# A GpSimd filler between row transfers, 128x256 or 128x512, with a new order of operations

## The chip, the core and the metric

The kernel runs on one core of one Trainium2 chip. The metric is the device time of one execution in microseconds (us). Seventeen executions of the kernel before the change have a median of 1318.66 us (1315.17 to 1323.75).

The engines are named as in the profile: PE is TensorE (matmuls), DVE is VectorE, ACT is ScalarE, POOL is GpSimd, and SP is the engine that issues the plain DMA transfers. Each engine works through its own queue of instructions in order and waits on semaphores for the others.

## What is computed

Two sequences of 2048 tokens with 128 features (4096 rows) go through a layer of the "macaron" kind: half a mixture of experts, a state-space block, half a mixture of experts.

```python
x = x + 0.5 * ffn(layernorm(x))      # mixture of experts, the first time
x = x + ssm(layernorm(x))            # selective state space: a scan over 2048 steps
x = x + 0.5 * ffn(layernorm(x))      # the same mixture, the second time

# ffn: 32 experts of 128x128, the 4 best of each row, and one shared expert of width 512
scores = softmax(flat @ router_w.T + router_bias)
topk_scores, topk_idx = top_k(scores, 4)
h = silu(flat @ gate_w[e].T) * (flat @ up_w[e].T);  out_e = h @ down_w[e].T
out = sum of the four chosen out_e, weighted with topk_scores
out = out + silu(flat @ sgate_w.T) * (flat @ sup_w.T) @ sdown_w.T

# ssm, 256 channels with 16 states each
h = h * exp(dt_t * A) + dt_t * u_t * B_t;  y_t = (h * C_t).sum(states) + D * u_t
```

## The kernel before

**Blocks and groups.** The 4096 rows are eight blocks of 512 rows, blocks 0 to 3 being the first sequence and 4 to 7 the second. A mixture takes groups of blocks: in the first mixture (0,1), (2,3) and (4,5,6,7), in the second (0,1,2,3), (4,5) and (6,7). Between them the state-space part goes through the blocks in order, since the states are carried on from block to block of a sequence.

**A mixture of a group.** DVE works out a place for each row at each of its four experts (the index tile `idx`, L855). POOL then scatters the rows to DRAM so that the rows of one expert lie together: an indirect DMA (L924) moves 128 rows at once, 4 x 4 of them for a block. These are the row transfers called *scatters* below; the DRAM tensors are `xs_100` for the first group of a layer's pair, `xs_102` and `xs_104` for the others. SP loads the sorted rows in chunks of 512 (`xs`, L1014), PE, ACT and DVE put each chunk through its experts (`pt_x` L1023, `gu` L1040, `h` L1065, `oq` L1078), and SP stores the result to DRAM (`ys`, L1091). Once all chunks of the group are stored, POOL *gathers* four results for each 128 rows into the tile `yg` (L1105, again an indirect DMA, 16 for a block), and PE adds them up with their weights (`sum`, L1130).

**A block of the state-space part.** After the projections, POOL forms `dt` and `dtu` in six products and sums of 128x512 (L1322 to L1324, called the *dt step* below, which waits for the logarithm of ACT at L1317). Then, for each of the 16 states, POOL multiplies `dtu` by a row of B (L1354, a *drive*, 128x1024), DVE scans twice (L1392) and multiplies by C (L1405), and PE adds the state up (L1171).

**The order.** Engines PE, DVE, ACT and SP run in the order in which the program is written out, and POOL's instructions are chained to the same order. That order is a list of 4504 operation numbers, `ORDER`, written into the file; `Plan.run` turns it into the order of emission. So the list decides what stands behind what in every queue.

**The filler.** Where more than two row transfers follow each other in POOL's order without other POOL work, `Plan.run` marks the third and every later one with `pause`, and `Plan.emit` then calls `pause()` ahead of it: POOL fills a tile named `pad`, which nobody reads, with zeros (L414). It is 128 partitions of 256 bf16 columns. There are 402 such fillers, called *pads* below.

Of the kernel before, what the change touches and what calls it, by code (L numbers as in the profile page):

```python
# [47 lines left out]
1 96 10 0 109 12 8 4-5 14 20 7 11 25 9 6 13 21 52 113 112 16 111 114-117 121-122 877 876 879 118-119 123-124 120  # L48
125-131 178 180 179 182-183 181 184-185 132 134 133 135-138 186-187 190 188-189 191-194 878 880 195 881 139 196-198
882 199 142 200 202 201 203-205 208 206 209 207 892 210 883 211 143 140 212 884 141 887 213 144-145 888-889 988-993  # L50
996 994-995 997 1000 998 1001 999 893 1002 894 1003 885 1004 39 18 26 22 17 24 19 15 98 27 29 28 23 40 46 34 2 94 3
73 79 72 93 85 35 48 32 104 59 31 45 44 63 110 88 82 77-78 49 102 494 56 92 84 886 1005 897 895-896 495 898-899 1006
1008 1007 1010-1011 1009 1012-1015 1018 1016 1019 1017 890 146 167 164 169 158 175 151 156 162 177 172-174 168 150
176 161 153 165 152 170 154 147-149 159 155 157 171 160 163 166 1020 900 1021-1022 496-497 891 901-902 498-499 903
1023 500 1024 1026 1025 1028-1030 904 906 1027 908 81 97 74-75 36 62 41 103 43 47 91 42 100 89 30 57 86 76 50 33 71
95 69 83 37 87 53 38 80 1031 905 907 909 108 214 90 105 228 242 70 51 68 215 442 216 106 66 256 1032-1033 1036 1034
1037 1035 1038-1039 910 912 1040 911 913-915 1041 217-220 229 221-223 230 224 243 916 244 231-232 225-226 233-235
257-258 917 236 245 237 246 238 247-248 259 249-250 260-261 239-240 270 64 58 61 227 241 60 67 284 65 298 251-252
262-264 560-562 271-272 253 563 920 265 254-255 266 273 276 285 274-275 277 286 267-268 278 921 279-280 287 290
288-289 291 281-282 292 918-919 922-923 293-294 299-300 54 312 326 269 564 295 566 296 503 565 567-568 570 569  # L60
572-573 571 574 504-505 575 501-502 301-302 506-507 303-304 313 305 327 306 314 307 576 508-511 328 512-513 308 577
315-316 318 317 340 354 368 283 309 319-320 310 341-342 514 321-322 516 515 517-518 578-579 582 580 583 581 519-520
584-587 590 588 591 589 592-593 521 329 332-333 330-331 334 594-595 55 382 311 297 323 355 324 356 335-336 343-348
369-370 337-338 325 396 339 101 349-350 357 360 358 361 359 362 351-352 363-364 1042-1045 524 1046 1048 1047
1049-1051 1054 1052 1055 1053 383 1056-1057 384 371 374 372-373 365 385 375 366 386 376-377 410 424 353 367 397
387-388 378 398 389 379 390 380 411 391 412 392 399-400 402 401 393 425 403 394 404-405 1058-1059 426 395 381 406
924 931 955 938 973 945 970 941 930 983 946 952 929 978 933 939 976 936 927 962 948 958-959 937 943 953 986 950 944
932 954 951 928 942 947 982 528 961 540 549 553 558 537 555 544 531 539 530 532 535 554 538 934 556 536 985 545 529
542 541 552 533-534 925 557 548 551 550 543 546 559 547 413 416 414-415 417-418 407-409 427 419 428-429 420 430-434
421 596 610 422 624 99 423 435-436 597 522-523 525 598 611-612 599-600 602 601 603-604 437 638 625-626 613 616  # L70
614-615 605 617-618 639 606-607 640 652 619 608 627-628 620 630-631 629 621 632 622 979 956 972 935 957 949 975 984
441 439-440 438 447-448 446 445 443 609 666 444 653 633 654 449 634 641 644 642-643 645-646 667-668 450-451 647-648
635 456 636 623 680 637 694 454 926 455 452-453 655 658 656 649 659 650 657 681-682 660-662 460 462 459 461 457-458
669 672 670-671 463 673 663 674 464 664 465 708 651 675 470 683-684 676 685-688 695 689 677 722 665 1508 696 690 678
1509-1510 691 709-710 692 1511-1512 467 977 468 476 466 474 473 981 475 469 940 697-699 1515 1513-1514 471 1516 472
700 477 701 1521 702 1522 703 723 1524 724 704 1528-1529 693 736 750 1523 764 679 478 1525-1526 711-712 479 714-715
713 1527 716 737-738 1530 705 717 706 1534 718 1535-1536 1531-1532 1542 707 778 1519 725 728 1537 526 1520 726 729
1538 968-969 967 965 487 490 489 482 481 488 971 483 480 1533 1539 1543 964 730 727 484 751-752 731 719-720 732
485-486 491 1544 492 527 493 1540 1545 739 742 740 1546 765 743 1547 741 744 766 1554 745-746 1548-1549 1555 721
1552 792 974 1553 1562-1563 733 1572-1573 963 753 756 1541 1556 734 754 1557-1558 755 757 735 806 758 1559 1564 1551  # L80
759 1565 1712 760 1550 779 747-748 780 1560 1566-1569 1574-1575 1582 749 1592 1517 767 770 1518 768 771 1576-1579
1584 769 772 1561 761-762 1586 1571 773 793 1585 774 1570 794 1602 1583 1593 1612 763 1587-1589 1594-1595 781
784-785 1580 782 1597-1598 807 1596 1581 1591 783 786 1599 1604-1605 808 1590 787 1600 788 775 1606 1603 980 1622
1632 795 1601 798 1607-1609 776 1614-1615 1613 1616-1619 1713 796 789 799 790 966 987 960 1060 777 1623 1633 1624
800 797 1611 801 1625 1714 809 1626-1629 812 1620 802 1610 1634-1635 1637-1638 803 1621 1636 1631 813 810-811 814
1639 1630 1644 804 1645 815-816 1642 1652 791 1662 1074 1646 1061-1062 1715 1643 817 1647-1649 1641 1075 1640 1654
1651 1653 1672 818 1657 1655 1658 1650 1716 1076 1664 1717 1665 1663 1667-1668 1674 1063 1656 1675 1673 1064 1659
1719 1666 1661 1677 1065 1669 1678 1718 1077 1720 1660 824 1078 1066-1067 1676 1068 1079 1088 805 1682 1692 819 1102
107 1679 1725 1732 1684 1670 1726 1685 1728 1069 1733 1070 1734 1683 823 829 820 830 821-822 828 827 1693 1686-1689
1727 1116 1746 1756 825 837 835 834 1071 1696 1671 1681 1089 1729 1694 1730 1735 1680 1736 1695 826 1072 1731 1090  # L90
831 1738 1697-1699 1766 1691 832 1737 836 1739-1740 1700-1701 1707-1708 1702-1703 1741-1742 838 833 842 1743 1747
841 843-844 1757 1709 1704 1080-1081 839-840 1082 1705 1710 845 1690 1748-1749 1706 1751 1711 1744 1758 1721 1723
1750 1745 1091 1752-1753 1722 1724 1092 1094 1754 1095 1759 1093 1761 1096 1767 1130 1776-1777 849-850 848 851
846-847 1083 852 1768 1916 1762 1103 1760 1763 1097 1084 1917 1769 1764 1098 1104 1918 1770-1773 1117 1755 1085 1765
1919 1778 1118 1779 1920 1086 1775 1780 1786 1796 1073 1787 1797 1781-1783 1788 1774 1789 1921-1923 1790 1105 1785
1791-1793 1924 1106 1798 1107 853 1799 1929 859 1930 1784 1794 854 1800-1803 1808 1936 1809 1932 1804 1937 1108 1810
1099-1100 1795 1806 1805 857 855 1807 1811-1813 1815-1817 858 1144 1826 1836 1931 1087 856 1818-1819 1933 1820-1823
1938 1119 1814 1934 1109 1120-1121 1939 1110 1935 1828 1111 1830 1827 860 1837 864 1101 1158 1846-1847 862 1942 1825
1829 1831-1833 861 1940 1112 1838 1131 1839 1824 1943-1944 1132 1840 1113-1114 1841-1843 1848-1849 1122 1133 1850
1145 1835 1845 1856 1941 863 865 1857 872 871 1851-1853 1945 1834 1134 1844 1123-1124 1135 1866 1115 1858 1125 1859  # L100
1946 1146 1126 1860-1863 1867 1876-1877 1868-1869 1871 1136 1855 1137 1127 1147 1870 1138 1150 1872-1873 1128 1148
1864 866 1854 1149 1151 867-868 1152 1878 1865 1159 1886 1172 1186 1879 1947-1948 1173-1174 1160 1139 1880 1896 1887
1153 1881-1883 1888 1140 1889 1874 1154 1884 1141 1890 1875 1891-1893 1142 1898 1161 1885 1900 1164 1899 873 869
1897 870 1901-1903 874 1894 1952 1950 1200 1951 1955 1162 1165-1166 875 1163 1904 1953 1895 1905 1954 1167 1175
1956-1957 1960 1129 1911 1906 1168 1962-1963 1178 1176 1179 1961 1970-1971 1214 1980 1143 1981 1965-1966 1177 1180
1972 1949 1155-1156 1990 1157 1964 1959 1967 1912-1913 1187-1188 1973 1181 1201 1974 1182 1202 1169 1975-1977 1968
1958 1982 1170 1983 1171 2000 2010 1228 1985-1986 1189-1190 1192 1907 1969 1193 1191 1194 1979 1984 1908 1987 1195
1992 1991 1995 2001 1196 1993 1996 1183 1215-1216 1184 1909 2002 1978 2005 1910 1197 1994 1203 1997 1206 1989 1400
# [1445 lines left out]
```

## Time and profile before

| what | value |
|---|---|
| median of 17 executions | 1318.66 us (1315.17 to 1323.75) |
| the profiled execution, its own time | 1320.99 us |
| its span, first to last instruction | 1319.2 us |
| mean granted TensorE clock in it | 0.91 |
| PE busy | 1051.9 us (80%) |
| POOL busy | 999.1 us (76%) |
| ACT busy | 896.8 us (68%) |
| DVE busy | 865.3 us (66%) |
| scatters, L924 (256) | 189.2 + 63.1 us, 985 and 986 ns each |
| gathers, L1105 (256) | 248.1 us, 969 ns each |
| pads, L414 (402) | 132.3 us, 329 ns each |
| drives, L1354 (128) | 303.3 us, 2380 ns each |

The shares of busy time are averages over stages with different limits. The first 300 us or so belong to the first mixture, whose experts of blocks 4 to 7 go on beside the state-space part; this one lasts from about 280 to 1030 us, with the second mixture's first group beside its second half; from there to the end the second mixture is alone. In a time line of the profile, a line gives the start, the duration, engine, source line, operation, what it writes and reads, and in brackets how long the engine had been idle before it and what ended that.

### The profile page before, as it was taken

The page shows a single profiled execution, that of the slowest core. Times are in us where ns is not written, and L with a number is a line of the kernel's source. Part 1 is how long each engine was busy: PE and PEld are TensorE (multiplying, and loading weights), DVE is VectorE, ACT ScalarE, POOL GpSimd, SP SyncE. Part 2 cuts the span into 40 slices and gives each one's busy share as a digit, 9 for nine tenths or more (in the row PEclk, how much of TensorE's full clock was granted, in tenths as well). Part 3 has the DMA queues.
Part 4 walks back from the last instruction along what each step waited for, and adds up shares of the span by engine and source line. Part 5 has one row for each costly group of instructions (what it writes and reads, how often), then busy time and mean ns, then how long its engine had stood idle before and what let it go on. Part 6 is the DMA issues. An engine that isn't in the chain of part 4 may idle for free.

```text
span 1319.2 us, 19281 instructions
## 1 busy us (share of the span) xinstructions
PE 1051.9 (80%) x5842; PEld 809.8 (61%) x5842; DVE 865.3 (66%) x1567; ACT 896.8 (68%) x1704; POOL 999.1 (76%) x1108
## 2 busy tenths in 40 slices
PE   6979956887876898886867666789787997968875
PEld 3657755666664775765535544556676886857754
DVE  7566511259989998994499999999997635212211
ACT  4536433699897999986777657477988656646632
POOL 1838888886898655658888899886657848888876
PEclk9989987888998899997989888779889997989897
DMA  9945324444424343431212222123344533555431
GB/s 311 347 156 177 110 86 130 119 111 136 123 82 111 98 121 114 114 105 44 62 59 72 65 80 87 52 73 91 94 122 134 148 110 100 165 142 142 123 104 52
DMA packets 186725, 154.10 MB, mean 117 GB/s; under 512 B 17665, under 2 KB 154498, under 8 KB 186626
## 3 DMA queue, kind: packets, MB, share of 16 engines
q1 hardware_dynamic: 170242, 119.29, 30.4%
q0 software_dynamic: 16384, 33.59, 9.1%
q8 instruction: 50, 0.82, 0.3%
q14 instruction: 49, 0.40, 0.1%
HBM read 89.64 MB, written 63.18 MB: 116 GB/s over the span
## 4 chain that ended last, share of the span: by engine, by line
PE 26%; DVE 25%; POOL 19%; ACT 15%; issue 8%; DMA 5%; POOLq 0%; DVEq 0%; SPq 0%; ACTq 0%
DVE hst L1392 11%; POOL yg L1105 7%; POOL xs L924 7%; PE gu L1040 6%; POOL pad L414 5%; ACT L420 4%; DVE hst L1405 4%; PE oq L1078 3%; ACT da L1366 3%; DMA yg<-ys,idx 3%; PE sum L1130 2%; PE gp L958 2%; PE pt_h L1023 2%; PE up L958 2%; PE y L1171 1%
## 5 line engine op out<-in xcount | busy, mean ns | idle before, releaser
L1354 POOL TENSOR_TENSOR hst<-dtu,bs 128x1024 f32<-128x1024 f32 x128 | 303.3, 2380 | 123.3 <-ACT st L1417 36.8
L1105 POOL DMA_INDIRECT yg<-ys,idx x256 | 248.1, 969 | 81.8 <-issue 39.9
L1392 DVE TENSOR_TENSOR_SCAN hst<-da,st,hst 128x512 f32<-128x512 f32 x192 | 238.0, 1269 | 13.7 <-ACT da L1366 9.5
L1040 PE MATMUL gu<-w_all,xT 128*128 x896 | 238.9, 406 | 9.7 <-ACT xT L1026 2.4
L924 POOL DMA_INDIRECT xs<-xn,idx x192 | 189.2, 985 | 62.9 <-issue 32.2
L1366 ACT ACTIVATE da<-dt,a 128x512 f32<-128x512 f32 x256 | 173.9, 691 | 61.7 <-DVE hst L1392 60.9
L1065 DVE TENSOR_TENSOR h<-sgq,gu 128x256 f32<-128x256 f32 x224 | 90.1, 416 | 167.1 <-ACT sgq L1059 166.6
L1040 PEld LDWEIGHTS gu<-w_all,xT 128*128 128x128 f32 x896 | 170.0, 203 | 48.2 <-issue 6.3
L420 ACT ACT_TABLE_LOAD x148 | 189.9, 1283 | 3.4 <-PEq L1542 0.8
L1171 PEld LDWEIGHTS y<-ident,hst 128*128 128x128 f32 x1024 | 127.3, 150 | 69.5 <-issue 42.7
L1405 DVE TENSOR_TENSOR hst<-hst,c 128x1024 f32<-128x1024 f32 x128 | 156.1, 1220 | 12.4 <-PE c L1378 3.9
L1171 PE MATMUL y<-ident,hst 128*128 128x128 f32 x1024 | 140.5, 288 | 15.6 <-DVE hst L1405 13.1
L1059 ACT ACTIVATE sgq<-gu 128x256 f32<-128x256 f32 x224 | 82.6, 383 | 73.7 <-PE gu L1040 57.1
L414 POOL MEMSET pad<- 128x256 bf16 x402 | 132.3, 329 | 0.2
L1130 PE MATMUL sum<-yg,dg 128*128 128x128 f32 x512 | 86.9, 314 | 56.9 <-DMA yg<-ys,idx 48.2
L1078 PE MATMUL oq<-w_all,hT 128*128 x896 | 123.6, 283 | 7.9 <-ACT hT L1073 7.0
L1078 PEld LDWEIGHTS oq<-w_all,hT 128*128 128x128 f32 x896 | 115.3, 198 | 19.7 <-ACT hT L1073 11.8
L1130 PEld LDWEIGHTS sum<-yg,dg 128*128 128x128 f32 x512 | 76.6, 219 | 73.2 <-issue 30.1
L1122 ACT ACTIVATE dg<-ident,wk 128x128 f32<-128x128 f32 x256 | 81.5, 391 | 50.5 <-PE sum L1130 50.4
L1023 PE MATMUL pt_h<-ident,h 128*128 128x128 f32 x448 | 75.2, 290 | 36.8 <-DVE h L1065 32.6
L1378 PE MATMUL c<-cm,pick 128*128 128x512 bf16 x128 | 52.3, 408 | 58.1 <-DVE hst L1405 58.0
L1023 PE MATMUL pt_x<-ident,xs 128*128 128x128 f32 x448 | 71.3, 285 | 33.6 <-DMA xs<-xs 27.1
(151 smaller groups left out, 1722.4 us busy)
## 6 DMA issues: line engine op xcount, KB each, us to landing
bs<-bd SPq DMA_DIRECT2D x128, 256.0 KB, 3.3
xs<-xs SPq DMA_DIRECT2D x112, 256.0 KB, 4.5
ys<-yq SPq DMA_DIRECT2D x112, 256.0 KB, 2.5
xs<-zero SPq DMA_DIRECT2D x56, 256.0 KB, 5.7
yg<-ys,idx POOLq DMA_INDIRECT x256
xs<-xn,idx POOLq DMA_INDIRECT x192
x<-in_x SPq DMA_DIRECT2D x8, 256.0 KB, 4.0
w_all<-in_up_w SPq DMA_DIRECT2D x8, 256.0 KB
```

Of the source, the lines that this page charges most:

```text
L414: pool(nc.gpsimd.memset(pad, 0.0))
L420: nc.scalar.preload_act_table_set(name)
L924: nc.gpsimd.indirect_dma_start(out=xs_b.t, out_offset=bass.IndirectOffsetOnAxis(ap=route["idx"][:, i * TB + t, k : k + 1], axis=0), in_=xn ...
L1040: nc.tensor.matmul(gu.t[:, s, :], xT.t[:, s0 + s, :], w_flat[:, bass.ds(offs["v"][s0 + s], 2 * H)], start=True, stop=True,)
L1078: nc.tensor.matmul(o.t[:, s, :], hT.t[:, s, :], w_flat[:, bass.ds(offs["v"][s] + 2 * H, D)], start=True, stop=True,)
L1105: nc.gpsimd.indirect_dma_start(out=yg.t[:, k, :], out_offset=None, in_=ys_b.t, in_offset=bass.IndirectOffsetOnAxis(ap=route["idx"][:, i * ...
L1130: nc.tensor.matmul(sm_.t, dg.t[:, k, :], yg.t[:, k, :], start=(k == 0), stop=(k == TOPK - 1),)
L1171: nc.tensor.matmul(y[:, t, k * P : (k + 1) * P], src[:, k, t * P : (t + 1) * P], ident.t, is_transpose=True, start=start and k == 0 and t ...
L1354: nc.gpsimd.tensor_tensor(h.t[:, :, 1:], dtu.t, bs.t.unsqueeze(1).to_broadcast([P, ND, T]), ALU.mult)
L1366: nc.scalar.activation(da.t, dt.t[:, k, :], AF.Exp, scale=a_t.t[:, k, s : s + 1])
L1392: nc.vector.tensor_tensor_scan(h.t[:, k, 1:], da.t, h.t[:, k, 1:], 0.0 if ini else st_sb[:, k, s : s + 1], ALU.mult, ALU.add,)
L1405: nc.vector.tensor_tensor(h.t[:, :, :T], h.t[:, :, 1:], cb.t.unsqueeze(1).to_broadcast([P, ND, T]), ALU.mult,)
```

## The change

Two things change. The pad is 512 columns wide instead of 256:

```diff
-    pad = const.tile([P, 256], BF16, tag="pad", name="pad")
+    pad = const.tile([P, 512], BF16, tag="pad", name="pad")
 
     def pause():
         pool(nc.gpsimd.memset(pad, 0.0))
```

And `ORDER` is another list of the same 4504 operations: nearly all of its lines differ, 4104 operations stand at another place, most of them near the old one. The new list has one line more, so that every source line below it is one higher.

```diff
 ORDER = """
-1 96 10 0 109 12 8 4-5 14 20 7 11 25 9 6 13 21 52 113 112 16 111 114-117 121-122 877 876 879 118-119 123-124 120
-125-131 178 180 179 182-183 181 184-185 132 134 133 135-138 186-187 190 188-189 191-194 878 880 195 881 139 196-198
+0 4 1 109 10 96 13 7-8 20 11 5 21 12 9 22 17 112 111 113 74 15 23 19 24 29 14 18 25 6 53 16 28 99 26-27 114-117
+121-122 879 877 876 118-119 123-124 120 125-128 130 129 131 178 180 179 181-185 132-133 135 134 136-138 186-194 878
...
```

What the new list does to POOL's queue, counted in the two programs' instructions, in the queue's order (a pad stands ahead of each third and later transfer of a row):

| stretch of POOL's queue | before | after |
|---|---|---|
| scatters of blocks 0 and 1 (`xs_100`) | 32, 31 pads | 32, 31 pads |
| transfers from the first scatter of blocks 4 to 7 (`xs_104`) to the first dt step | 121, 120 pads | 114, 113 pads |
| of these, up to the 16th gather, which completes block 0 | 97 | 89 |
| scatters among the first drives of block 0 | 7 | 14 |
| 32 gathers of blocks 2 and 3, among drives and dt steps | 10 pads | 9 pads |
| gathers between the last drive of block 3 and the dt step of block 4 | 41, 39 pads | 43, 41 pads |
| transfers among the drives of blocks 4 to 7 | 13 pads | 12 pads |
| scatters of blocks 4 and 5 in the second mixture | 12, a drive, 20; 29 pads | 32, a drive; 30 pads |
| from the first gather of blocks 0 to 3 in the second mixture to the end | 31 gathers, 32 scatters, 97 gathers; 158 pads | 30 gathers, 1 scatter, 2 gathers, 31 scatters, 96 gathers; 158 pads |
| pads in all | 402 | 396 |

In PE's queue, the two totals of the routing of blocks 4 to 7 (`tot` L769, `rest` L790) still stand behind the first transposes of sorted rows (`pt_x`, L1023), but now with one of the shared experts' products (L958) in between instead of four.

In SP's queue the first transfers change places too: the loads of `x`, the weights and the clearing of the DRAM rows are in another order, and the first scatter still stands behind all 16 clearings of `xs_100`.

## The prediction

> **What bounds the kernel now.** I read the page first (busy shares, then the chain of work that ended last), then POOL's time line where stages begin and end, and last the busy time of each engine by stretches.
>
> ```profile
> PE 26%; DVE 25%; POOL 19%; ACT 15%; issue 8%; DMA 5%; POOLq 0%; DVEq 0%; SPq 0%; ACTq 0%
> ...
> L414 POOL MEMSET pad<- 128x256 bf16 x402 | 132.3, 329 | 0.2
> ```
>
> No engine owns the chain: it changes hands. So I look for the stretches in which POOL's row of transfers is what the others wait for.
>
> ```profile
> core 0: us, PE busy (x) PEld busy (x) DVE busy (x) ACT busy (x) POOL busy (x), PEclk, DMA share, GB/s
> 96.00:275.00 179.00, 146.88 (x815) 115.49 (x813) 60.40 (x174) 90.06 (x185) 156.79 (x242) 0.90 0.44 130
> ...
> 591.00:654.00 63.00, 48.60 (x224) 33.85 (x223) 27.29 (x74) 44.03 (x90) 52.19 (x81) 0.86 0.20 55
> 663.00:912.00 249.00, 178.69 (x808) 118.87 (x807) 236.02 (x287) 167.07 (x288) 214.43 (x157) 0.84 0.22 68
> 1071.00:1311.00 240.00, 195.39 (x1175) 163.62 (x1173) 63.64 (x201) 128.58 (x309) 205.06 (x319) 0.91 0.43 118
> ```
>
> The columns are the stretch, its length, the busy time of PE, weight loads, DVE, ACT and POOL, the granted clock, the DMA's share and rate. In 96 to 275, POOL is idle for 22.2 us of 179, and 121 transfers with an issue gap of 0.165 us each (below) make 20.0 of them: it is full. So it nearly is in 591 to 654 and in 1071 to 1311, while in 663 to 912 DVE is (95%). POOL's time line at the end of the first stretch:
>
> ```profile
> 270.29 1.01 POOL L924 DMA_INDIRECT xs<-dtu,idx  x1 [0.17 <-issue]
> 271.30 0.33 POOL L414 MEMSET pad<- 128x256 bf16 x1
> 271.79 0.97 POOL L1105 DMA_INDIRECT yg<-ys,idx  x1 [0.16 <-issue]
> 272.75 0.33 POOL L414 MEMSET pad<- 128x256 bf16 x1
> 273.24 0.95 POOL L1105 DMA_INDIRECT yg<-ys,idx  x1 [0.16 <-issue]
> 275.00 1.26 POOL L1322 TENSOR_TENSOR w<-w,ea 128x512 f32<-128x512 f32 x1 [0.80 <-ACT w L1317]
> ```
>
> One place in a row is 0.95 transfer + 0.33 pad + 0.16 gap = 1.44 us for a gather, 1.455 for a scatter. The dt step at 275.00 stands right behind the row and waits only 0.80 us more, for ACT; with it the state-space part begins. The row is the bound, with the data hardly later. The same holds at 653.95, the dt step of block 4: its logarithm (L1317) ends at 653.48 and the gather ahead of it at 653.93. And it holds to the end: the last of 160 transfers is issued at 1310.14, and the span ends 9 us later.
>
> **The change part by part: the pad.** No row shows a 512-column fill on POOL. The rows by shape are 101 ns for 128x16 bf16 (the tile pick), 194 and 202 for 128x128 bf16, 206 for 128x128 f32, median 325 for 128x256. So it goes by columns, not bytes: 127 ns for the last 128. 256 more columns cost 254 ns at that slope, 222 at the slope from 16 to 128 columns (97 ns for 112), and 325 if the whole instruction doubles. I take 0.25 us, nearest the last two rows, and keep 0.22 and 0.325. The gap stays: it is 0.16 behind a 2.4 us drive as behind a 0.33 us pad, so a longer pad doesn't hide it. The Trainium skill (GPSIMD Engine Reference, 3.1 and 1) has 1.03 cycles for an element of a simple body at 1.2 GHz, an estimate of 0.22 us for 256; the trace's 127 ns for 128 columns says 0.25, and by the page the sum below would be some 10 us smaller.
>
> I see nothing that a longer pad gives back: a transfer takes a median of 965 (scatter) or 951 ns (gather) against means of 985 and 969, so all irregularity in 512 of them is about 10 us.
>
> **Start to the first dt step.** The 31 pads of the first scatters add 31 x 0.25 = 7.8 us before blocks 0 and 1 are out. POOL itself then idles until the index of blocks 4 to 7:
>
> ```profile
> 96.23 0.96 POOL L924 DMA_INDIRECT xs<-dtu,idx  x1 [21.02 <-DMA xs<-xs]
> ```
>
> The page names a DMA, but L855 on DVE ended at 95.48, and that chain starts at tot on PE (85.48), which is queued behind pt_x, which waited for the scattered rows (79.34, idle 5.89). So the 7.8 us do reach it. Four products (80.22 to 85.48) stood between pt_x and tot, 5.3 us; now one does, some 1.6. Net +4.1: the row starts at 100.3. Its 121 transfers took 178.0 us (96.23 to 274.19, 1.471 each); 114 take 167.7, plus 113 x 0.25 = 28.3, that is 196.0. The row ends at 296.3 and the step begins there, against 275.00: **+21.3**. The 16th gather, which block 0's data wait for, was at 238, 37 us ahead of the step; now it is 89 places of 1.72 us into the row, at 253.5, so the data are ready at 290.5 and the row remains the later one. The seven scatters that moved behind it (7 more unpadded ones among the drives, some 8 us of POOL) I cost at **0**: POOL waited 13 us in 296 to 341 (for st, L1417, and DVE); uncovered they cost 8.
>
> **State space.** Nine pads among the gathers of blocks 2 and 3, with POOL 90.35 of 102 us busy there: 9 x 0.25 = **+2** (0 to 2.3). Then the row ahead of block 4: 41 x 0.25 = 10.3, two more gathers of 1.69 = 3.4, less the waits for yg's two buffers (1.81, 1.03, 1.03 us, the usual 0.16 taken off: 3.4), which a slower row outwaits: **+10** (10 to 13.7). Twelve pads among the later drives, 3.0, where DVE is the bound: **+2** (0 to 3).
>
> **The tail.**
>
> ```profile
> 1071.59 0.98 POOL L1105 DMA_INDIRECT yg<-ys,idx  x1 [17.93 <-DMA ys<-yq]
> ...
> 1118.16 1.00 POOL L924 DMA_INDIRECT xs<-xn,idx  x1 [0.54 <-DVE ej L866]
> ...
> 1249.54 0.95 POOL L1105 DMA_INDIRECT yg<-ys,idx  x1 [2.52 <-PE sum L1130]
> ...
> 1265.55 0.95 POOL L1105 DMA_INDIRECT yg<-ys,idx  x1 [4.66 <-DMA out_y<-x]
> ```
>
> The 30 pads of the scatters before it (7.5 us) fall into the 17.93 us wait for the experts of blocks 0 to 3. But the last drive now stands behind all 32 scatters: its end comes 32 x 1.705 + 2.4 = 57 us after the row's start instead of 19.4 (1005.29 to 1024.68), and on DVE the experts' products (L1065) of the last chunks are queued behind its scans, with the experts' results and so the gathers behind them. In the trace DVE came to these scans 43.5 us after the row's start (1048.76); three more products are now ahead of them, at some 2.4 us each (20 of them stood between 1005 and 1053, scans among them), which makes 51. So the drive is some 6 us late, of which I take **+4** (0 to 12). From the first gather on, 158 x 0.25 = 39.5 us, less the four stalls inside that stretch (1.20 at 1113.46 and the last three shown, 0.16 off each: 8.3): **+31.2** (31.2 to 39.5). The scatters of blocks 6 and 7 end some 16 us later, their experts too, but the row itself is 24 us late by then, so it stays ahead.
>
> Sum: 21.3 + 0 + 2 + 10 + 2 + 4 + 31.2 = **+70.5**. The profiled span is 1319.2 us and its execution's own time 1320.99, 2.3 above the median; added to the median of 1318.66 the sum gives **1389 us**.
>
> **A rule against the change.** The time spent waiting for pads is, by the profile, PE 2.5 us, weight loads 5.3, DVE 0.2. The Trainium skill (SBUF — State Buffer, Who interferes with whom) says that a GpSimd instruction holds a port pair shared with VectorE for its whole length and that VectorE's copy and tensor_scalar in a two-port mode block meanwhile. By the 0.2 us it adds nothing; by the rule a dozen such steps in the last routing could each wait 0.25 us longer, an estimate of 3 us.
>
> **Rivals.** *The order covers one of the two long rows* (first: only 89 transfers ahead of block 0's data instead of 97, and DVE is busy 60 of 179 us there, so work could be drawn forward and DVE's 4 to 9 idle us per hundred later used up). Then the +21.3 and the +14 of the state space go: 1389 - 35 = 1354. Against it: the dt step still stands behind 114 transfers.
>
> *Faster.* The new list closes DVE's gaps in the state space. From 330 to 1030 DVE is busy 613.6 of 700 us, so 86 are idle. A list that wins more than 70 of them decides; all of them give 1389 - 86 = 1303. Against it: 44 of the 86 lie in 530 to 730, around the gather row that grows by two transfers and 41 longer pads, and the rows on POOL can't shrink below their count.
>
> *Worse.* The pad doubles to 0.65 us (333 pads on the path x 0.075 = +25), the moved scatters cost 8 and the late last drive 8 more: 1389 + 41 = 1430, or 1410 with half of that. For it: the last drive's place; against it: the column slope.
>
> *The pad is no longer than before* (only the list acts): near 1319. The step from 128 to 256 columns speaks against it.
>
> **How the numbers follow.** The forecast (1367 to 1405: 10 us down for a pad of 0.22 more, 8 up for stalls that are not outwaited, and some 10 either way for DVE's gaps under another list) 0.60; one row covered 0.17; worse 0.12; faster 0.08; no change 0.03. So slower 0.89, same 0.03, faster 0.08; 0.2%, 2.6 us, is about what a measurement of this kernel can tell from no change. The range, 1345 to 1416, takes in the forecast, most of the covered row and half of the worse case.
>
> **What would show it.** A pad row of 0.55 to 0.6 us and a pitch of 1.69 to 1.71 us in the rows; the first dt step at 293 to 300 us; some 76 us from the end of block 3's last drive to the dt step of block 4 instead of 66.4 (587.59 to 653.95); the last 160 transfers taking about 270 us instead of 239.5. I am wrong if the first dt step comes before 285, if the stretch from 663 on shortens by over 20 us, or if PE and not POOL ends the tail.

## The result, and the profile after

| what | before | after |
|---|---|---|
| median | 1319.14 us (47 executions) | 1375.7 us (1370.48 to 1378.98, 8 executions) |
| ratio to the kernel before | 1 | 1.0421, 95% interval 1.0401 to 1.0442 |
| span of the profiled execution | 1319.2 us | 1373.5 us |
| pads | 402 of 0.325 us (median) | 396 of 0.538 us |
| scatter, gather, medians | 0.965, 0.951 us | 0.965, 0.950 us |

The change makes the kernel 4.2% slower. From the page of the kernel after, the shares of the chain of work that ended last ("issue" is time in which an engine waited for nothing that the profile shows) and the pads' group:

```profile
POOL 35%; DVE 24%; PE 18%; issue 10%; ACT 7%; DMA 6%; SPq 0%; POOLq 0%; DVEq 0%; ACTq 0%
...
L415 POOL MEMSET pad<- 128x512 bf16 x396 | 215.6, 545 | 0.3
```

POOL has 35% of the chain where it had 19%. The pads grew by 83 us in all (132.3 to 215.6), and the span by 54.3. The stretches of the kernel after, cut at the same landmarks as in the prediction (first long row, row ahead of block 4's dt step, blocks 4 to 7 of the state space, scatters of blocks 4 and 5, the tail):

```profile
core 0: us, PE busy (x) PEld busy (x) DVE busy (x) ACT busy (x) POOL busy (x), PEclk, DMA share, GB/s
100.00:294.00 194.00, 148.40 (x828) 117.64 (x827) 63.66 (x182) 94.77 (x191) 173.19 (x228) 0.89 0.42 120
611.00:683.00 72.00, 58.66 (x252) 39.88 (x252) 29.36 (x78) 41.73 (x95) 62.72 (x84) 0.79 0.18 51
683.00:1023.00 340.00, 256.74 (x1315) 184.85 (x1315) 325.03 (x457) 248.79 (x426) 276.14 (x186) 0.86 0.28 82
1023.00:1096.00 73.00, 61.24 (x391) 53.40 (x390) 27.06 (x50) 43.04 (x82) 49.39 (x63) 0.93 0.48 138
1096.00:1365.00 269.00, 203.12 (x1176) 170.17 (x1173) 68.17 (x211) 128.43 (x308) 237.64 (x318) 0.89 0.38 105
```

The tail took 240 us with POOL busy 205; now it takes 269 with POOL busy 238, and PE's work in it is much the same (195 and 203). POOL fills these rows as before, only with longer pads. And POOL's time line where the first row ends:

```profile
291.28 0.98 POOL L925 DMA_INDIRECT xs<-dtu,idx  x1 [0.17 <-issue]
292.26 0.54 POOL L415 MEMSET pad<- 128x512 bf16 x1
292.96 0.98 POOL L1106 DMA_INDIRECT yg<-ys,idx  x1 [0.16 <-issue]
293.98 1.26 POOL L1323 TENSOR_TENSOR w<-w,ea 128x512 f32<-128x512 f32 x1
```

The first dt step (last line) starts without any idle time behind the last gather: the row's length alone sets it. From start to start this place of the row takes 1.68 us (292.96 minus 291.28). The median of all such places is 1.67 us for a scatter and 1.65 for a gather, against 1.46 and 1.44 before.

### The profile page after: what moved, and what is told of

Read it like the earlier page. It is cut to its first block, busy times and chain, and to the rows that moved or that the text cites. A ratio compares the mean times of both kernels' runs of the same rounds, so it can differ in the third digit from the quotient of the medians.

```text
span 1373.5 us, 19311 instructions
## 1 busy us (share of the span) xinstructions
PE 1061.2 (77%) x5842; PEld 817.8 (60%) x5842; DVE 855.1 (62%) x1567; ACT 884.3 (64%) x1694; POOL 1083.1 (79%) x1102
## 4 chain that ended last, share of the span: by engine, by line
POOL 35%; DVE 24%; PE 18%; issue 10%; ACT 7%; DMA 6%; SPq 0%; POOLq 0%; DVEq 0%; ACTq 0%
DVE hst L1393 12%; POOL pad L415 11%; POOL yg L1106 10%; POOL xs L925 10%; PE gu L1041 4%; DVE hst L1406 4%; POOL hst L1355 2%; PE y L1172 2%; DMA yg<-ys,idx 2%; PE oq L1079 2%; ACT L421 2%; ACT da L1367 2%; DMA xs<-xs 2%; PE pt_x L1024 1%; PE sum L1131 1%
## 5 line engine op out<-in xcount | busy, mean ns | idle before, releaser
L1041 PE MATMUL gu<-w_all,xT 128*128 x896 | 234.7, 401 | 7.9 <-ACT xT L1027 2.6
L415 POOL MEMSET pad<- 128x512 bf16 x396 | 215.6, 545 | 0.3
L1131 PE MATMUL sum<-yg,dg 128*128 128x128 f32 x512 | 91.7, 322 | 70.3 <-DMA yg<-ys,idx 60.8
L1079 PE MATMUL oq<-w_all,hT 128*128 x896 | 127.5, 289 | 4.4 <-ACT hT L1074 3.1
L1079 PEld LDWEIGHTS oq<-w_all,hT 128*128 128x128 f32 x896 | 119.8, 204 | 14.6 <-ACT hT L1074 6.8
L1027 ACT COPY xT<-pt_x 128x512 f32<-128x512 f32 x112 | 65.1, 584 | 70.6 <-PE pt_x L1024 69.7
L1024 PEld LDWEIGHTS pt_x<-ident,xs 128*128 128x128 f32 x448 | 55.0, 147 | 80.1 <-issue 59.4
```

Of the source, the lines that this page charges most:

```text
L415: pool(nc.gpsimd.memset(pad, 0.0))
L1041: nc.tensor.matmul(gu.t[:, s, :], xT.t[:, s0 + s, :], w_flat[:, bass.ds(offs["v"][s0 + s], 2 * H)], start=True, stop=True,)
L1079: nc.tensor.matmul(o.t[:, s, :], hT.t[:, s, :], w_flat[:, bass.ds(offs["v"][s] + 2 * H, D)], start=True, stop=True,)
L1131: nc.tensor.matmul(sm_.t, dg.t[:, k, :], yg.t[:, k, :], start=(k == 0), stop=(k == TOPK - 1),)
```

## The experiments

Each ratio is to the kernel before on the same chip in the same set of runs, where it had medians of 1323.92 us (e1 to e4), 1389.84 (e5 to e8) and 1323.43 (e9 to e12).

### The two parts apart (e1, e2)

Pad alone, old order (e1):

```diff
-    pad = const.tile([P, 256], BF16, tag="pad", name="pad")
+    pad = const.tile([P, 512], BF16, tag="pad", name="pad")
```

> The old order with the pad of 512 columns. Theory (the longer pad costs its length wherever POOL's row is what the rest waits for): the pad is 0.538 us instead of 0.325, so 0.213 more. First dt step: 120 pads and a start 6.6 us later, 275 + 32 = 307; the row ahead of block 4 some 5 more, the 13 later pads 3, the last 160 transfers 33.7 less up to 8.3 of stalls, 25 to 31. Sum +65 to +71: 1384 to 1390, so slower than with the new order (1375.7). Rival (the new order is what costs, and the old one hides the pads): under 1345.

Measured: 1397.92 us, ratio 1.0567 (1.0524 to 1.0610). That is 8 us above the expected range; against the kernel before on the same chip it is +74 us where +65 to +71 was expected. The wide pad costs 74 us in the old order, as much as 347 of the 402 pads at 0.213 us each.

New order alone, the pad left at 256 columns (e2): the changed kernel with

```diff
-    pad = const.tile([P, 512], BF16, tag="pad", name="pad")
+    pad = const.tile([P, 256], BF16, tag="pad", name="pad")
```

> The new order with the old pad of 256 columns. Theory: the first row has 114 transfers instead of 121, so the first dt step comes some 10 us earlier (265, if the data of block 0 are ready by then); the stretch from the dt step of block 4 to the scatters of blocks 4 and 5 keeps the 12 us that it won; the late last drive costs little. 1297 to 1312, faster than before. Rival (the new order is the worse one and costs part of the 4%): 1325 to 1350.

Measured: 1298.22 us, ratio 0.9815 (0.9772 to 0.9857), within the expectation. So the new order by itself is *better* than the old one, by 26 us. The product of the two ratios is 1.037, against 1.042 for both together: within the intervals, the parts add. The same stretches in the kernel with the new order alone:

```profile
91.00:260.00 169.00, 144.53 (x815) 114.73 (x814) 63.08 (x181) 92.89 (x188) 148.15 (x228) 0.94 0.46 134
575.00:641.00 66.00, 55.38 (x254) 38.11 (x253) 29.39 (x78) 41.56 (x95) 54.91 (x84) 0.84 0.21 55
641.00:980.00 339.00, 255.37 (x1310) 184.72 (x1312) 324.76 (x457) 248.29 (x426) 272.34 (x185) 0.86 0.29 82
980.00:1048.00 68.00, 62.14 (x396) 54.33 (x397) 28.12 (x53) 43.77 (x83) 43.23 (x65) 0.95 0.51 148
1048.00:1288.00 240.00, 198.34 (x1169) 166.46 (x1169) 67.05 (x209) 127.92 (x308) 204.40 (x318) 0.91 0.43 118
```

Line by line against the kernel after, the pad lengthens the stretches in which a row fills POOL (169 to 194, 66 to 72, 240 to 269) and the one in which a row of scatters stands ahead of the last drive (68 to 73), and leaves the one that DVE fills alone (339 and 340). Against the kernel before, the order shortens mainly two: this last one, from 351 us (654 to 1005) to 339, and the first row, which has seven transfers fewer, from 179 to 169.

The same cut at exact landmarks, from the profiles of five kernels (us):

| stretch | before | e1, pad | e2, order | after | e9, new order, 16 columns |
|---|---|---|---|---|---|
| first scatter to 33rd (31 pads) | 68.2 | 74.9 | 62.8 | 71.4 | 59.3 |
| to the first dt step (120 pads, new order 113) | 178.8 | 203.5 | 168.6 | 193.5 | 149.5 |
| to the end of block 3's last drive (11) | 312.6 | 313.0 | 312.3 | 314.2 | 311.1 |
| to block 4's dt step (39; 41) | 66.4 | 72.2 | 68.9 | 75.3 | 63.0 |
| to the scatters of blocks 4 and 5 (13; 12) | 351.3 | 356.1 | 339.2 | 339.6 | 343.7 |
| to the second mixture's first gather (29; 30) | 66.3 | 71.9 | 67.6 | 73.3 | 60.8 |
| to the last gather's end (159; 158) | 239.5 | 269.1 | 239.9 | 269.2 | 216.4 |

### The pad taken away (e3, e4)

No pad at all, old order (e3):

```diff
-            if o.pause:
-                pause()
             o.fn()
```

> The old order without any pad (nothing is computed differently, pad is read by nobody). Theory: a place in a row falls from 1.44 to some 1.25 us (0.95 transfer and the 0.30 gap that two adjacent transfers show now), 0.19 less. First dt step -23 at most, less where the data are later; row of block 4 -2; tail -30 at most, but there the experts come to be the bound: 1270 to 1300. Rival (the pads keep something from backing up that the trace of before can't show): transfers of well over 0.97 us or gaps over 0.3 us in the rows, and 1319 or more.

Measured: 1275.06 us, ratio 0.9639 (0.9596 to 0.9683), as expected. POOL's time line in its tail:

```profile
1211.20 0.94 POOL L1103 DMA_INDIRECT yg<-ys,idx  x1 [2.06 <-DMA yg<-ys,idx]
1212.44 0.94 POOL L1103 DMA_INDIRECT yg<-ys,idx  x1 [0.30 <-issue]
1213.69 0.94 POOL L1103 DMA_INDIRECT yg<-ys,idx  x1 [0.30 <-issue]
```

Without a pad the gap between two transfers is 0.30 us, and a place takes 1.25.

A pad of 16 columns, old order (e4):

```diff
-    pad = const.tile([P, 256], BF16, tag="pad", name="pad")
+    pad = const.tile([P, 16], BF16, tag="pad", name="pad")
```

> The old order with a pad of 16 columns, 0.10 us. Theory: a place is 0.95 + 0.10 + 0.16 = 1.21 us, the shortest of all; within 5 us of the kernel without pads. Rival (the length of the pause matters, not that there is an instruction): as slow as without pads, over 1319, if that is slow; if without pads is fast, this is the same.

Measured: 1262.27 us, ratio 0.9535 (0.9493 to 0.9576): 13 us *below* e3 instead of level with it, though the pad took 0.130 us and not 0.10. The expectation failed, and the traces show one reason that has nothing to do with the pad's length: the pads also tie the scatters of a row to one order. (In the program a scatter is chained to POOL's other work, pads included, but not to other scatters.) Without them the first 48 scatters of the third group (`xs_104`) all came ahead of the 32 of the second (`xs_102`), instead of 36 ahead and 12 mixed with them, the loads of the second group's sorted rows came at 191.9 us instead of 182.9, and the first gather had to wait 8.9 us. So e3 isn't a clean test of the pad, and e4 is the better one. In this stretch, up to the first dt step, e3's trace is 10.7 us longer than e4's (168.7 and 158.0); that all of the 13 us has this cause isn't shown.

### A set that can't be read (e5 to e8)

Four more kernels, the first with a 16-column pad in the new order (e5); the second with 512 columns until the first drive and 256 from there (e6, against the kernel after); the third with 256 columns until 127 drives are issued and 512 from there (e7, `drives[0] > 126` in the same place); the fourth with 256 columns, the old order up to the first dt step of block 4 and the new one behind it (e8, as e12 below):

```diff
+    drives = [0]
     def pause():
-        pool(nc.gpsimd.memset(pad, 0.0))
+        pool(nc.gpsimd.memset(pad if drives[0] == 0 else pad[:, :256], 0.0))
...
             def drive(bs=bs, h=h):
+                drives[0] += 1
```

> The new order with a pad of 16 columns. Theory (a place in a row costs its length, and what the new order won with the 256 pad, 1.85%, it wins with a short one too): old order with this pad was 0.9535 of before, so 0.936 to 0.945, some 1237 to 1248. Rival (the new order's gain rests on the long rows, which are shorter here): no better than the old order with this pad, 0.95 to 0.957.

> The new order; the pad writes 512 columns up to the first drive and 256 from there on. Theory: between the two traces of the new order the first dt step moves from 259.9 to 294.0, and nothing later gives that back since DVE is the bound behind it: 1298 + 34 = 1332 (1326 to 1338). Rival (DVE's gaps in the state space take much of a late start back): 1300 to 1318.

> The new order; the pad writes 256 columns until 127 drives are done and 512 from there on, so in the scatters of blocks 4 and 5 of the second mixture and in the last 160 transfers. Theory: 158 pads x 0.213 = 33.7 less some stalls, 29.7 between the traces, and up to 6 for the last drive, which stands behind 30 wide pads: 1298 + 30 to 36 = 1328 to 1334. Rival (the experts on PE bound the tail too): under 1320.

> Pad of 256 columns; the old order up to the first dt step of block 4, and from there the new one. Theory (the new order wins twice: 13 us up to that step, and 12 us between it and the scatters of blocks 4 and 5): the second gain stays, 0.989 to 0.993 of before. Rival (all of it comes from the early part): 0.998 to 1.002.

Measured: e5 1511.55 us, ratio 1.0927 (1.0839 to 1.1015); e6 1367.9, 0.9871 (0.9820 to 0.9922); e7 1377.56, 0.9930 (0.9902 to 0.9959); e8 1387.32, 0.9954 (0.9911 to 0.9997). But on this chip the kernel before took 5% longer than on the others, and the traces show a disturbance that the kernels' own work doesn't explain. One example, ACT's copy of the first group's normalised rows, in e8:

```profile
48.85 0.59 ACT L650 COPY xnT<-pt_n 128x512 f32<-128x512 f32 x1 [6.95 <-remote]
```

The same instruction starts at 43.96 in the kernel before, after 2.56 us behind PE. Here it waits 7 us for a releaser that the profile doesn't have ("remote"), while PE and DVE stand still too. In e5 such a wait is far longer (the columns are the sum, the number and the longest):

```profile
DVE x L997 <- remote: 66.4, 3, 53.8
```

Over the whole span, DVE and ACT wait 130 to 394 us for "remote" or "issue" in these four runs and 0 to 5 us in e1 to e4; the packets of the transfers took as long as elsewhere (a median of 84 ns for plain ones of 2 KB in all; in the queue of the indirect ones a mean of 111 to 119 ns, and 111 to 118 elsewhere). What held the engines up stays open. Nothing is concluded from these four, and the first three were run again.

### The same again (e9 to e11), and half of the order (e12)

> The new order with a pad of 16 columns once more, because in the run e5 the engines stood 394 us behind waits that nothing in the trace releases (DVE and ACT together; 1 to 8 us in the first four runs), so that its time cannot be read. If the order's gain (0.9815 at 256 columns) adds to that of the short pad (0.9535): 0.933 to 0.940 of the kernel before. If the order only pays with long row transfers: 0.948 to 0.960. If e5's slowness was the kernel's own: above 1.05 again, with DVE and ACT once more behind more than 200 us of waits without a releaser.

> The new order with 512 columns up to the first drive and 256 after it, once more for the same reason (DVE and ACT stood 130 us behind waits without a releaser in e6). If the wide pad is paid in full in the part ahead of the first dt step (293.98 us against 259.90 with the narrow one, +34): 1326 to 1334 us where the kernel before takes 1319, a ratio of 1.005 to 1.012. If the later part gives some of it back: 0.985 to 0.998.

> The new order with 256 columns until 127 drives are done and 512 from there, once more. If the last 160 transfers pay about 0.2 us each and nothing else moves (269 us from the second layer's first gather to the end against 248 in the kernel before): 1323 to 1334 us, a ratio of 1.003 to 1.011, and with e10 the two parts add up to nearly the whole of after minus order alone (+75 us of span). If other work hides it: below 1.000.

Measured: e9 1242.53 us, ratio 0.9384 (0.9348 to 0.9419); DVE and ACT wait 4 us for "issue" and nothing for "remote", so e5's slowness was not the kernel's own. The order's gain adds to the short pad's (0.9815 x 0.9535 = 0.936). This is the best version of the study, 6% faster than the kernel before and 10% faster than the changed one. Its page gives the chain as

```profile
PE 37%; DVE 25%; ACT 14%; POOL 11%; issue 8%; DMA 4%; SPq 0%; POOLq 0%; DVEq 0%; ACTq 0%
```

and its time line shows a place of a gather row with the 16-column pad:

```profile
1199.52 0.95 POOL L1106 DMA_INDIRECT yg<-ys,idx  x1 [0.18 <-issue]
1200.47 0.12 POOL L415 MEMSET pad<- 128x16 bf16 x1
1200.77 0.95 POOL L1106 DMA_INDIRECT yg<-ys,idx  x1 [0.18 <-issue]
```

POOL is down to 11% of the chain; the tail of 216 us has PE busy for 192 of it.

e10: 1331.61 us, ratio 1.0060 (1.0033 to 1.0086). e11: 1336.81 us, ratio 1.0108 (1.0068 to 1.0148). Both ratios fell as the first theory has it (e11's at its upper end, its time 3 us above): the wide pad is paid mostly where it stands. (The 248 us in e11's expectation run to the end of the span; to the last gather's end, as the 269 do, it is the 239.5 of the table.) Over the order alone (0.9815), the first 144 wide pads cost 0.0245 (32 us) and those behind the last drives 0.0293 (39 us), 0.0538 together of the 0.0606 between e2 and the kernel after. In e11's trace, the two stretches with the wide pads are 35 of these 39 us longer than in e2 (67.6 to 73.4, 239.9 to 269.1). Neither has wide pads between the first drive and the 127th; of the pads there, the row ahead of block 4 costs 6.3 us (68.9 to 75.3 in the table).

A pad of 16 columns with the old order up to the first dt step of block 4 and the new one behind it (e12):

```diff
-    pad = const.tile([P, 256], BF16, tag="pad", name="pad")
+    pad = const.tile([P, 16], BF16, tag="pad", name="pad")
...
-2327 3123 1457-1458 3124 2334 3128 1460 1462 1467 2333 2335-2336 3129-3130 2512 2337 3232 2513 3131-3132 3233 2338
+2327 3123 1457-1458 3124 2334 3128 1460 1462 1467 2333 2512 3129-3130 1463-1465 1469 1466 2335-2337 3232 3131-3132
...
```

> A pad of 16 columns, the old order up to the first dt step of block 4 and the new one from there. If the new order's gain of about 12 us in the second half is its own (the DVE steps of blocks 4 to 7 meet fewer drives and ACT loads fewer tables): 0.943 to 0.947, and better than 0.9535. If it needs the new order's first half or the long pads: 0.951 to 0.957. If the order's whole gain at a short pad comes from the second half, this ties with e9 within 4 us.

Measured: 1257.02 us, ratio 0.9527 (0.9485 to 0.9569), in the range of the second theory: by its time, no gain over e4 (0.9535) that these intervals could show, and e9 is 14 us better; the third theory's tie with e9 is out. In the stretch itself the trace does show the gain, as the first theory has it: 346.2 us from block 4's dt step to the scatters against 358.1 in e4. The two profiles exaggerate the rest: e12's was taken in its fastest execution, e4's in its slowest (spans of 1251.3 and 1268.3). What the second half of the order is worth by itself stays open: by the two ratios at most some 9 us. That the whole order is worth more at this pad than its second half follows from e9.

### What the order does in the state space

This wasn't isolated by a kernel; it is read from ten traces. From block 4's dt step to the scatters of blocks 4 and 5 the old order takes 351.3 to 358.1 us (before, e1, e4; e3 354.7), the new one 339.2 to 343.7 (e2, after, e9, e10, e11) and 346.2 (e12), whatever the pad. DVE runs 456 to 460 operations there in all of them. I counted those that took over 1.4 times the shortest of the same operation on the same tiles: 45 with 48.0 us too much before, 37 with 38.5 after; 42 to 45 with 44.6 to 52.7 us in the old order, 37 to 39 with 37.8 to 43.4 in the new one. That is 9 of the 12 us. Nearly all of the excess, 43.6 us before and 34.6 after, is in operations that ran at the same time as one of POOL's products; the others have 4.4 and 3.9. The new list also spares ACT six loads of its function tables in this stretch (58 to 52), the other reason that the expectation of e12 names; but DVE waited for ACT's `da` only 3.2 us there before and 1.5 after, so this can account for little. Here is one of the slowed operations before, on DVE and then on POOL:

```profile
700.24 3.63 DVE L1270 TENSOR_TENSOR cm<-bc,cm 32x512 bf16<-32x512 f32 x1
703.89 0.69 DVE L1308 SCALAR_TENSOR_TENSOR ea<-w,ea 128x512 f32<-128x512 f32 x1
```

```profile
699.92 0.99 POOL L1105 DMA_INDIRECT yg<-ys,idx  x1 [0.16 <-issue]
700.94 2.38 POOL L1354 TENSOR_TENSOR hst<-dtu,bs 128x1024 f32<-128x1024 f32 x1
703.48 1.27 POOL L1105 DMA_INDIRECT yg<-ys,idx  x1 [0.17 <-issue]
```

L1270 takes 0.69 us undisturbed; here a drive (L1354) begins 0.70 us after it, and it ends 0.55 us behind the drive. For the three DVE lines L1255, L1270 and L1308, which all take 0.69 us undisturbed, over the whole span:

| | touches a POOL product (L1322 to L1324, L1354) | touches none (pads and transfers included) |
|---|---|---|
| before | 17: medians 3.27, 2.32 and 1.45 us, at most 4.63 | 15: at most 0.69 |
| after | 13: medians 1.83, 2.67 and 1.55 us, at most 4.72 | 19: at most 0.69 |

The scans (L1392), one of whose two inputs, `da`, lies in PSUM and not in SBUF in this program, don't suffer (a median of 1.26 us with a product beside them or without), and no pad, of 256 or 512 columns, does it to these three lines. The Trainium skill (SBUF — State Buffer, Who interferes with whom) has this case: a VectorE instruction with two inputs in SBUF contends with a GpSimd instruction that reads SBUF, and not with one that only writes it. The rows agree on both halves: the drives read, the pads only write. By the table, moving such an operation from beside a drive to beside a transfer saves up to 4 us of DVE, by the medians 0.8 to 2.6, where DVE is the bound.

## Why the prediction was right, and where its sizes were off

The direction and the mechanism held: POOL's rows are the bound in three stretches, and the wide pads in them are nearly all paid: 69.7 us more than in e2, where 343 pads at 0.213 are 73.1. 1375.7 lies 13 us under the 1389 forecast, inside the range. Term by term, on the span:

| term | forecast | measured | of it order (e2) | of it pad (after minus e2) |
|---|---|---|---|---|
| to the first dt step | +21.3 | +19.0 | -15.1 | +34.1 |
| moved scatters, gathers of blocks 2 and 3 | +2 | +1.6 | -0.3 | +1.9 |
| row ahead of block 4's dt step | +10 | +8.9 | +2.6 | +6.3 |
| later drives, late last drive | +6 | -4.8 | -10.8 | +6.0 |
| the tail | +31.2 | +29.7 | +0.4 | +29.2 |
| sum (the measured ones of the unrounded terms) | +70.5 | +54.3 | -23.2 | +77.6 |

**The pad's price.** 0.25 us was too much: 0.538 minus 0.325 is 0.213, a little under the lower bound of 0.22, and the slope is 0.83 ns a column from 256 to 512 and 0.81 from 16 to 256 (0.130 us). The step from 128 to 256 columns, which I took as the nearest, overstates it, because its two rows weren't alike: the 128-column ones are single fills at the program's start, and such a fill is shorter than a pad of the same shape (101 ns for the 128x16 tile pick, 130 for the 128x16 pad of e4 and e9). Of the two slopes, the one from 16 to 128 columns, which the forecast gave as 222 ns, was nearer. So was the estimate of 0.22 from the Trainium skill (GPSIMD Engine Reference, 3.1). The 343 pads of the three POOL rows are 12.7 us cheaper for it, though part of this came back: the first 33 transfers took 8.6 us more than in e2, where 31 x 0.213 is 6.6, and the tail's stalls shrank only from 8.3 to 5.0 us instead of to nothing. These two are what is left of the tail's:

```profile
1298.72 0.95 POOL L1106 DMA_INDIRECT yg<-ys,idx  x1 [2.16 <-PE sum L1131]
...
1313.29 0.95 POOL L1106 DMA_INDIRECT yg<-ys,idx  x1 [3.17 <-PE sum L1131]
```

So the tail is 158 x 0.213 = 33.7 less 3.3, or 30.4, against 29.7 measured; and "the gap stays" held (0.16 behind the 512-column pad as behind that of 256).

**Start to the first dt step.** The row started at 100.46 (100.3 forecast) and the dt step at 293.98 (296.3). That the start fits so well is partly luck: the order alone moved it by -4.9 us (91.33 in e2, against 96.23; -3.7 forecast) and the wide pads by +9.1 from there (+7.8 forecast). From the measured start, with 113 pads at the true price, the working gives 292.2; the rest is a row that is 0.9 us longer than forecast with the narrow pad (168.6 in e2) and pads at 0.22 each. The moved scatters cost nothing, as said (312.6 and, in e2, 312.3).

**The failed term** is "**+2**" and "**+4**" for blocks 4 to 7. The pads' part of it was right (+6.0 for 6), and the last drive is as late as was said: it ends 54.7 us after the scatters' start (57 forecast) and not 19.4, though its place alone costs only 1.3 us (66.3 to 67.6) and the 30 pads before it 5.7. What I missed is that the new list makes the DVE-bound stretch 12 us shorter (351.3 to 339.2). I had counted only DVE's idle time there as something to win, and took its busy time as fixed. The trace of before had the rows that say otherwise: L1255 and L1270 at means of 1.88 and 1.50 us, with a shortest of 0.69.

**The rivals.** *The order covers one long row*: no, the rows are paid in full (e10, e11), and the dt step still stands directly behind its row. *Faster*: right that the list wins time in the state space, some 11 us of the 70 it needed, though mostly by shorter operations of DVE and not by closing its gaps. *Worse*: the price went the other way (and its 333 pads on the path should have been 343, as in the sum). *The pad is no longer*: no. And the rule that I weighed against the change, VectorE's copies and tensor_scalar blocked by pads, did act, if for little time. In the kernel after, the index of the last group is one of its cases:

```profile
1141.68 0.54 POOL L415 MEMSET pad<- 128x512 bf16 x1
1141.71 0.54 DVE L856 TENSOR_SCALAR idx<-p 128x32 uint32<-128x32 f32 x1
...
141.15 0.20 DVE L856 TENSOR_SCALAR idx<-p 128x32 uint32<-128x32 f32 x1
```

The same operation took 0.20 us where it ended just ahead of a pad (last line). Five such copies and tensor_scalar operations that met a wide pad took 0.22 to 0.45 us longer than their shortest, 1.7 us in all, and three of them ended 0.03 to 0.05 us behind the pad; with the narrow pads of e2 it is 0.6 us in all. In the last routing it comes to 0.8 us of the 3 estimated. The 0.2 us that I set against the rule count waits ahead of an operation, and this time is inside it.

## What to carry to other kernels

When an engine's row of work is the bound, a filler in it is paid at nearly its full length, so try it at its shortest before searching an order around it; here 16 columns kept the one order that the filler enforced at 8 ns a place, and were worth 4.7% (e4). An edit and a newly searched order should be timed apart: here the order's gain of some 25 us hid nearly a third of a loss of 78, and both numbers were needed to see that the best version has the one without the other. Where an engine is busy throughout, its time isn't fixed: compare the mean and the shortest time of each kind of its operations, and look at what runs beside the long ones.

## What the runs showed of the hardware that I had not expected

- A 16-column fill between two indirect transfers costs almost nothing: from start to start a scatter's place takes a median of 1.271 us with it (e9) and 1.263 without (e3), a gather's 1.257 and 1.249, since the gap of 0.305 us between two transfers shrinks to 0.178 behind the fill of 0.130.
- The three DVE operations of 0.69 us that read two tiles of SBUF took up to 4.7 us beside POOL's products (5.6 in e9), and at most 0.74 beside pads and indirect transfers. Copies and tensor_scalar did meet the pads: 0.54 us instead of 0.20 for one beside a 512-column pad.
- On one chip, engines stood for up to 53.8 us with no releaser in the trace, and the same kernel (e5, e9) took 1511.55 us there and 1242.53 on another.
- The granted clock in the stretch of the first long row was 0.89 after, 0.90 before, 0.94 in e2 and 0.99 in e9, each from one execution; no run here explains it.
